# Layer norm of the first half rewritten, two-input sums redistributed over VectorE and GpSimd, and a new order of steps

## The chip, the cores and the metric

The kernel runs on one core of one Trainium2 chip, as a single launch. The metric is device time in microseconds (us) from the start to the end of the execution. The time of the kernel before is the median of 3 runs, 2762.42 us (2761.38 to 2765.03). All views of the profile come from one more execution, which took 2765.32 us.

## The reference, cut to what matters

There are 64 graphs of 256 nodes with 512 features. Everything is fp32: x is [64, 256, 512], adj [64, 256, 256], nodemask [64, 256], and each weight matrix has 512 rows. Two residual layers follow each other, each ended by a layer norm:

```python
def _gcn_layer(x, adj, W, b):
    return adj @ (x @ W) + b
h = relu(_gcn_layer(x, adj, W1, b1))
h = relu(_gcn_layer(h, adj, W2, b2))
x = _layernorm(x + _gcn_layer(h, adj, W3, b3))      # first half

q, k = jnp.split(x @ Wqk, 2, axis=-1)
v = x @ Wv
agg = adj @ (k * mask[:, :, None])
w = inv_scale * mask * (q * agg).sum(-1)            # one score for each node
x = _layernorm(x + softmax(w, axis=1)[:, :, None] * v)   # second half
```

`_layernorm` subtracts the mean of a row and divides by the root of its variance plus 1e-5; it has neither gain nor offset.

## The kernel before

*Pairs and products.* The graphs are handled as 32 pairs (`NPAIR`; `PAIR` = `G` = 2). Every large product is one level of a Strassen-Winograd scheme with seven products in place of eight: `seven` (L104) gives their order, 1, 7, 6, 2, 5, 4, 3, and says which PSUM bank each goes into and which sums are made after it. What the products need as operands are sums and differences of quarter blocks. These are the many small two-input operations of the kernel. The products from PSUM are combined by VectorE (`add`, L53; `sub`, L56) after ScalarE has copied one of the two to a buffer `tmp` (L109), or after `add` has made that `tmp` with another operand.

*Where the two-input sums run.* `unit` (L62) sends a sum to VectorE if its name is in the list `ON_DVE`, to GpSimd otherwise. A name is the owner and the number of the sum: h17 is S7 of layer 1's output (made from hT after the relu), h23 is S3 of layer 2's output, c2T6 and c2T7 are sums of the second layer's `support` results (buffers `sup`), x3, x5, x6 and x7 the sums S of the next pair's xT, and x4 to x7 also the sums T of the masked xm; a3 to a7 are sums of the adjacency, b3 the sum of x and the third layer's bias.

*The stages of a pair.*

- F, `front`: three times `support` (L290, the activations by W) and between them `aggregate` (L331, the adjacency), with bias and relu on ScalarE (L322) and the first sums S of the relu's result after it (`a_sums`). At its end it issues the loads of the mask and of x (1 MB, L85).
- S, `sums`: the three sums S of the next pair's xT, the four sums x + b3 (x<-x,b3b), the four sums of the next adjacency.
- B, `back`, for the pair before: the third aggregation (`adj_times`, L367), which makes the residual r and its statistics (mvt holds mean and variance); then `inv_std` (L371), the layer norm, the transposition of r in blocks of 32 x 32 by VectorE (L488, buffer tr), its way over DRAM (tr to via, via to x1T: five DMAs), and the sums T of xm (`t_sums`).
- G, `gather`: the adjacency by xm, into gt. M, `attention`: four copies and sums Z of x1T, the sums I of those on GpSimd (L59), and 49 products (L546) with blocks of Wv and of M = Wq Wk^T. These come from DRAM through a ring of seven buffers; the next fetch is issued after each product. The results R are combined by VectorE, v<-R makes v, and `score` (L563) makes w from gt.
- E, `finish`, for the pair before that: the softmax, v = v * s + r (L603), statistics, layer norm (ScalarE, L619) and the two stores out<-v (L622).

*What sets the order.* The kernel is written as generators, each of which gives a piece of its stage at a time. The loop over i = 0 to 32 interleaves F and S of pair i, B, G and M of pair i - 1 and E of pair i - 2. Which generator gives its next piece is a string of letters written by hand: `START` for i = 0, `ORDER` for i = 1 to 30, `LAST` for 31 and `END` for 32. With `manual_schedule` each engine's queue (TensorE, VectorE, ScalarE, GpSimd, and SyncE, which issues all DMAs) holds its instructions in the order in which they are written. So a string decides what stands ahead of what on every engine.

*The layer norm of the first half.* `inv_std` returns rs, one over the root of the variance, and nb = -mean * rs. From these `back` makes mrs = rs * ISCALE * mask and mnb = nb * ISCALE * mask. For each of the four (h, g) blocks of 128 x 512, ScalarE writes xm = r * mrs + mnb to another buffer (L460), and VectorE then turns r in place into r * rs + nb (L462), which may only overwrite r when ScalarE has read it. In the last pair (`end`) r is transposed by TensorE (L478), after 20 warming matmuls, and not over DRAM.

*Buffers that the text speaks of.* x and xm share one buffer (tag "x", one copy), R takes the places of T, x1T and Z, there is one v, two hT, five tmp, nine sup, six S and eight PSUM banks.

Of the kernel before, what the change touches and what calls it, by code (L numbers as in the profile page):

```python
# [9 lines left out]
FP = mybir.dt.float32  # L10
AF = mybir.ActivationFunctionType
OP = mybir.AluOpType
AX = mybir.AxisListType

P = 128
PAIR = 2
G = PAIR
# [3 lines left out]
def gcn_then_graph_attention(ctx: ExitStack, tc: tile.TileContext, xT, xN, adjT, mask, W1, b1, W2, b2, W3, b3,  # L21
                             WqT, WkT, Wv, out):

    nc = tc.nc
    NPAIR = xT.shape[0]
    N, D = 256, 512
    NH, DC = N // P, D // P
    HD = D // 2
    EPS = 1e-5
    ISCALE = 1.0 / math.sqrt(D)  # L30
# [1 line left out]
    SUP = 9  # L32
    SBUFS = 6
    TMP = 5
    ON_DVE = ('a5', 'c2T5', 'c2T6', 'c3T6', 'c3T7', 'h13', 'h23', 'h27', 'x3', 'x5')

    const = ctx.enter_context(tc.tile_pool(name="const", bufs=1))
    pool = ctx.enter_context(tc.tile_pool(name="work", bufs=1))
    small = ctx.enter_context(tc.tile_pool(name="small", bufs=2))
# [12 lines left out]
    def add(o, a, b):  # L52
        nc.vector.tensor_tensor(o, a, b, op=OP.add)  # L53
# [7 lines left out]
    def unit(name, o, a, b, op=OP.add):  # L61
        (nc.vector if name in ON_DVE else nc.gpsimd).tensor_tensor(o, a, b, op=op)  # L62

# [307 lines left out]
    def inv_std(mvt, n=G):  # L371

        sd = small.tile([P, NH, n], FP, name="sd")
        nc.scalar.activation(sd, mvt[:, :, :, 1], AF.Sqrt, bias=eps)  # L374
        rs = small.tile([P, NH, n], FP, name="rs")
        nc.vector.reciprocal(rs, sd)  # L376
        nb = small.tile([P, NH, n], FP, name="nb")
        nc.vector.scalar_tensor_tensor(nb, mvt[:, :, :, 0], -1.0, rs, op0=OP.mult, op1=OP.mult)  # L378
        return rs, nb

    def softmax_rows(w, gs):

# [50 lines left out]
    def back(i, C, aS, x, mask_t, end, put):  # L433
        r = pool.tile([P, G, NH, D], FP, name="r", tag="xT" if end else "r", bufs=1)
        xb = lambda h, j: x[:, :, h, j * HD:(j + 1) * HD]
        rb = lambda h, j: r[:, :, h, j * HD:(j + 1) * HD]
        st = small.tile([P, NH, G, 6], FP, name="st")
        mvt = small.tile([P, NH, G, 2], FP, name="mvt")

        def block(o, a, b, h=None):  # L440
            add(o, a, b)
            if h is not None:
                for g in range(G):
                    nc.vector.bn_stats(st[:, h, g], r[:, g, h, :])
                for g in range(G):
                    nc.vector.bn_aggr(mvt[:, h, g], st[:, h, g])
        yield from adj_times(aS, C, lambda y, t: add(rb(0, 1), y, t), lambda x: block(rb(0, 0), x, xb(0, 0), 0),
                             lambda v, t: block(rb(1, 1), v, t, 1), lambda v, t: add(rb(1, 0), v, t),
                             plus=(xb(0, 1), xb(1, 1), xb(1, 0)))

        rs, nb = inv_std(mvt)
        yield
        mrs = small.tile([P, NH, G], FP, name="mrs")
        nc.vector.scalar_tensor_tensor(mrs, rs, ISCALE, mask_t, op0=OP.mult, op1=OP.mult)
        mnb = small.tile([P, NH, G], FP, name="mnb")
        nc.vector.scalar_tensor_tensor(mnb, nb, ISCALE, mask_t, op0=OP.mult, op1=OP.mult)
        xm = pool.tile([P, G, NH, D], FP, name="xm", tag="x", bufs=1)

        def apply(h, g):
            nc.scalar.activation(xm[:, g, h, :], r[:, g, h, :], AF.Identity, scale=mrs[:, h, g:g + 1],  # L460
                                 bias=mnb[:, h, g:g + 1])
            nc.vector.tensor_scalar(r[:, g, h, :], r[:, g, h, :], rs[:, h, g:g + 1], nb[:, h, g:g + 1],  # L462
                                    op0=OP.mult, op1=OP.add)
        hg = [(h, g) for h in range(NH) for g in range(G)]
        xmb = [[xm[:, :, h, j * HD:(j + 1) * HD] for j in range(2)] for h in range(2)]
        if end:
            warm(20)
            x1T = [pool.tile([P, 2, G, N], FP, name="x1T", tag="act", bufs=2) for _ in range(2)]
            x1b = lambda h, k: x1T[k][:, :, :, h * P:(h + 1) * P]
            for h, g in hg:  # L470
                apply(h, g)
            yield
            xS = t_sums(xmb)
            for h, g in hg:
                yield
                pt = bank((P, 2, 2, P))
                for c in range(DC):
                    nc.tensor.transpose(pt[:, c // 2, c % 2], r[:, g, h, c * P:(c + 1) * P], ident)  # L478
                for k in range(2):
                    (nc.scalar.copy if h else nc.vector.tensor_copy)(x1T[k][:, :, g, h * P:(h + 1) * P], pt[:, k])  # L480
        else:
            tr = pool.tile([P, 4, 32, NH, 2, 2, G], FP, name="tr", tag="gt", bufs=1)
            x1T = pool.tile([P, P, NH, 2, 2, G], FP, name="x1T", bufs=1)
            x1b = lambda h, k: x1T[:, :, h, k].rearrange("p n c g -> p c g n")
            for h, g in hg:
                apply(h, g)
                for k in range(2):
                    nc.vector.transpose(tr[:, :, :, h, k, :, g].rearrange("p q j c -> p c q j"),  # L488
                                        r[:, g, h, k * HD:(k + 1) * HD].rearrange("p (c q j) -> p c q j", c=2, q=4))
                yield  # L490
            via = dram.tile([4, P, D], FP, name="via")
            nc.sync.dma_start(via.rearrange("q p e -> p q e"), tr.rearrange("p q j h k c g -> p q (j h k c g)"))
            for q in range(4):
                nc.sync.dma_start(x1T[q * 32:(q + 1) * 32].rearrange("p (a j) h k c g -> p a (j h k c g)", a=4),
                                  via[q].rearrange("(a i) e -> i a e", a=4))
            yield
            xS = t_sums(xmb)
        yield
        gt = pool.tile([P, NH, G, D], FP, name="gt", tag="gt", bufs=1)
        gb = lambda h, j: gt[:, h, :, j * HD:(j + 1) * HD]  # L500

        def gather():
            steps = adj_times(aS, xS, lambda y, t: add(gb(0, 0), y, t), lambda x: nc.scalar.copy(gb(0, 1), x),
                              lambda v, t: add(gb(1, 0), v, t), lambda v, t: add(gb(1, 1), v, t))
            for n, _ in enumerate(steps):
                if n == 6:
                    put["gt"] = gt
                    if i + 2 < NPAIR:
                        aTs[i + 2] = load_adj(i + 2)
                yield  # L510
        put["G"] = gather()
        w = small.tile([P, NH, G], FP, name="w", bufs=2)
        put["M"] = attention(i, x1b, w, r, mask_t, put)
# [80 lines left out]
    def finish(i, prev, gs=range(G)):  # L594

        r, v, w = prev
        n = len(gs)
        softmax_rows(w, gs)
        yield
        s = softmax_cols(gs)  # L600
        for k, g in enumerate(gs):
            for h in range(NH):
                nc.vector.scalar_tensor_tensor(v[:, g, h], v[:, g, h], s[:, h, k:k + 1], r[:, g, h, :],  # L603
                                               op0=OP.mult, op1=OP.add)
        yield
        st = small.tile([P, NH, n, 6], FP, name="st")
        mvt = small.tile([P, NH, n, 2], FP, name="mvt")
        for k, g in enumerate(gs):
            for h in range(NH):
                nc.vector.bn_stats(st[:, h, k], v[:, g, h])  # L610
                yield
        for k in range(n):
            for h in range(NH):
                nc.vector.bn_aggr(mvt[:, h, k], st[:, h, k])  # L614
        rs, nb = inv_std(mvt, n)
        yield
        for k, g in enumerate(gs):
            for h in range(NH):
                nc.scalar.activation(v[:, g, h], v[:, g, h], AF.Identity, scale=rs[:, h, k:k + 1],  # L619
                                     bias=nb[:, h, k:k + 1])  # L620
                yield
            nc.sync.dma_start(out[i, :, g * NH * D:(g + 1) * NH * D].rearrange("p (h f) -> p h f", h=NH), v[:, g])  # L622

    ORDER = ("BBFEFFBEBFBFBFBFFFBEFFFFBFSFBBBFFFBBBFGFFGGFFGFEEGMFFGMMMEGMMSFFMEMMEMMEFESMMEEFFMSM"
             "SMMMFMMMMFFEMMMMMMMMSMMMMMMFSMMMSSMMSSM")
    START = ("FFFBFBBFFBFBBBBBFFFFFFBBBBBFBBBBBBBBBBBFFBBBBSBFFBSBFBBFFFBBFBBFBFSFBFFBBBBFBBSFFBSB"
             "BSFBSFFSBBBSBBBBBSFBBBBBSBSBB")
    LAST = ("FBBSEFBFEBBFFBFBFBFFBFFFFEBBFFBBFBFBEFEEGFEGGFFEGEFFMMGSFFGMMMMFEFMMMMEMMMMMMEMMMFMM"
            "GSMMMMEMMMMMMMMFMMMSSMMMFMSSSFMFFSFSFSM")
    END = ("BEBBBBBBEBBBBBBBBGMGMEMMBEGGEEMGEGEMMMMMMEMEEMEMMMMMMMMMMMGMMBMMMMMMMMMMXMMXXMMMXYXM"  # L630
           "XMYXYMYYMYXYMYXYBMYMMXXYYXM")

    def run(order, rest, **gens):
        res = {}
# [81 lines left out]
```

## Time and profile before

| | |
|---|---|
| median of 3 runs | 2762.42 us (2761.38 to 2765.03) |
| the profiled execution | 2765.32 us |
| its span, first to last instruction on the core | 2763.5 us |
| mean TensorE clock granted, as a share of the full one | 0.996 |
| instructions | 41007 |
| DMA | 403.7 MB, 146 GB/s on the mean |
| VectorE transposes tr<-r (L488) | 248, 606 ns each |
| GpSimd sums x<-x,b3b (L62) | 128, 1523 ns each |
| GpSimd sums sup<-sup (L62) | 160, 1372 ns each |
| VectorE sums R<-ps,tmp (L53) | 384, 616 ns each |
| ScalarE copies tmp<-ps (L109) | 768, 584 ns each |

The engines are PE (TensorE's matmuls), PEld (its loading of weights, beside the matmuls), DVE (VectorE), ACT (ScalarE), POOL (GpSimd) and SP (SyncE, which issues DMAs; SPq is its queue). A group of instructions is written as line, engine, operation, output<-inputs. A timeline line gives the start in us from the start of the span, the us from the first start to the last end, the group and how many instructions it holds, and in brackets the idle time of the engine just before it with what ended it. A waits line gives the group that waited, what ended the wait, and the total, the times and the longest, in us. [...]

### The profile page before, as it was taken

What the parts mean: (1) busy time and instruction counts of PE and PEld (TensorE: products, weight loads), DVE (VectorE), ACT (ScalarE), POOL (GpSimd) and SP (SyncE); (2) the same over time, 40 slices, a digit from 0 to 9 for tenths busy, and PEclk for the clock granted to TensorE, in tenths of its full rate; (3) what the DMA queues carried; (4) which work ended last, traced back from release to release, by engine and by line L of the source; (5) the groups of instructions that cost most, each with busy time, mean ns of one, the idle gap of its engine ahead of it and who ended that gap; (6) DMA issues with size and microseconds to landing.
All of it is one profiled execution on the core that took longest, in us unless ns stands there. A gap on an engine that the chain in (4) does not pass through costs nothing. (4 is left out here: it accounts for less than half of the span.)

```text
span 2763.5 us, 41007 instructions
## 1 busy us (share of the span) xinstructions
PE 2716.9 (98%) x14290; PEld 2401.7 (87%) x14290; DVE 2145.0 (78%) x3828; ACT 1133.1 (41%) x2050; POOL 1262.8 (46%) x966
## 2 busy tenths in 40 slices
PE   9999999999999999999999999999999999999996
PEld 8888888888888888888888888888888888888885
DVE  5778777877777777778777777877787877778777
ACT  3434344434344343443334443434433444434343
POOL 3535455444554354544445543445544455434442
PEclk9999999999999999999999999999999999999998
DMA  6534554344544445543455444455434554434553
GB/s 209 165 110 147 165 175 135 117 143 154 163 151 123 126 147 162 173 135 112 143 162 162 141 129 131 147 162 176 133 115 141 161 162 148 130 123 147 162 155 97
DMA packets 202233, 403.71 MB, mean 146 GB/s; under 512 B 24752, under 2 KB 61872, under 8 KB 193968
## 3 DMA queue, kind: packets, MB, share of 16 engines
q1 hardware_dynamic: 202032, 401.10, 46.5%
q8 instruction: 117, 1.92, 0.3%
q14 instruction: 84, 0.69, 0.1%
HBM read 328.54 MB, written 72.48 MB: 145 GB/s over the span
## 5 line engine op out<-in xcount | busy, mean ns | idle before, releaser
L109 ACT COPY tmp<-ps 128x512 f32<-128x512 f32 x768 | 431.3, 584 | 643.3 <-PE ps L290 257.1
L62 POOL TENSOR_TENSOR sup<-sup 128x512 f32<-128x512 f32 x160 | 218.1, 1372 | 565.9 <-DVE sup L53 409.2
L546 PE MATMUL ps<-ring,I 128*128 128x256 f32 x1792 | 433.0, 381 | 7.7 <-DVE tmp L53 3.0
L546 PEld LDWEIGHTS ps<-ring,I 128*128 128x128 f32 x1792 | 334.1, 190 | 66.3 <-DVE R L53 11.7
L290 PE MATMUL ps<-w_T,S 128*128 128x256 f32 x1536 | 351.0, 381 | 9.2 <-POOL S L62 7.6
L301 ACT COPY sup<-ps 128x512 f32<-128x512 f32 x96 | 56.2, 586 | 722.2 <-PE ps L290 722.2
L290 PEld LDWEIGHTS ps<-w_T,S 128*128 128x128 f32 x1536 | 286.7, 190 | 59.7 <-POOL S L62 20.5
L546 PE MATMUL ps<-ring,Z 128*128 128x256 f32 x1344 | 327.9, 380 | 1.1 <-ACT Z L524 1.1
L59 POOL TENSOR_TENSOR I<-Z 128x384 f32<-128x384 f32 (+1 forms) x128 | 190.1, 1504 | 244.5 <-DVE Z L527 150.8
L546 PEld LDWEIGHTS ps<-ring,Z 128*128 128x128 f32 x1344 | 254.4, 190 | 38.4 <-ACT Z L524 3.3
L331 PEld LDWEIGHTS ps<-aT,sup 128*128 128x128 f32 x2048 | 253.5, 192 | 13.2 <-issue 6.6
L331 PE MATMUL ps<-aT,sup 128*128 128x128 f32 x2048 | 261.8, 276 | 1.8
L53 DVE TENSOR_TENSOR R<-ps,tmp 128x512 f32<-128x512 f32 (+1 forms) x384 | 221.2, 616 | 48.7 <-PE ps L546 48.4
L62 POOL TENSOR_TENSOR x<-x,b3b 128x512 f32<-128x512 f32 x128 | 192.2, 1523 | 128.7 <-DMA x<-in_xN 119.3
L290 PE MATMUL ps<-w,hT 128*128 128x256 f32 x1024 | 242.0, 379 | 0.0
L290 PE MATMUL ps<-w_T,hT 128*128 128x256 f32 x1024 | 236.5, 379 | 0.0
L290 PEld LDWEIGHTS ps<-w_T,hT 128*128 128x128 f32 x1024 | 194.6, 190 | 26.5
L53 DVE TENSOR_TENSOR sup<-ps,tmp 128x512 f32<-128x512 f32 x288 | 192.8, 677 | 30.8 <-PE ps L290 30.7
L290 PEld LDWEIGHTS ps<-w,hT 128*128 128x128 f32 x1024 | 192.0, 190 | 24.7
L331 PE MATMUL ps<-aS,sup 128*128 128x128 f32 x1536 | 206.3, 279 | 1.7 <-ACT tmp L109 1.1
L322 ACT ACTIVATE hT<-hT,b 128x256 f32<-128x256 f32 x384 | 167.4, 501 | 87.1 <-DVE hT L53 86.2
L331 PEld LDWEIGHTS ps<-aS,sup 128*128 128x128 f32 x1536 | 188.9, 192 | 11.4 <-DVE hT L53 4.8
(116 smaller groups left out, 4762.8 us busy)
## 6 DMA issues: line engine op xcount, KB each, us to landing
ring<-mv SPq DMA_DIRECT2D x672, 256.0 KB, 3.6
x<-in_xN SPq DMA_DIRECT2D x32, 1024.0 KB, 8.0
out<-v SPq DMA_DIRECT2D x64, 512.0 KB, 7.6
xT<-in_xT SPq DMA_DIRECT2D x31, 1024.0 KB, 5.0
via<-tr SPq DMA_DIRECT2D x31, 1024.0 KB, 4.2
x1T<-via SPq DMA_DIRECT2D x124, 256.0 KB, 4.7
ring<-mv SPq DMA_DIRECT2D x224, 128.0 KB, 3.1
aT<-in_adjT SPq DMA_DIRECT2D x32, 512.0 KB, 3.9
```

What stands on the lines that cost most here:

```text
L53: nc.vector.tensor_tensor(o, a, b, op=OP.add)
L59: (nc.gpsimd).tensor_tensor(o, a, b, op=op)
L62: (nc.vector if name in ON_DVE else nc.gpsimd).tensor_tensor(o, a, b, op=op)
L109: nc.scalar.copy(t, ps)
L290: nc.tensor.matmul(ps[:, g], lhsT=src[n][:, c, g], rhs=w[n][:, c], start=(first and g == 0 and c == 0), stop=(g == G - 1 and c == 1), skip ...
L301: nc.scalar.copy(C[2], x)
L322: nc.scalar.activation(o[:, c], (o if ps is None else ps)[:, c], AF.Relu, bias=b[:, 2 - 2 * j + c:3 - 2 * j + c])
L331: nc.tensor.matmul(ps[:, c, g], lhsT=C[n][:, g, c * P:(c + 1) * P], rhs=aS[n][:, g], start=(first and c == 0 and g == 0), stop=(c == 1 and ...
L546: nc.tensor.matmul(ps[:, k], lhsT=left[n](place[o]), rhs=wt[:, k], start=(first and k == 0), stop=(k == len(outer) - 1), skip_group_check= ...
```

## The change

The layer norm's second form: VectorE first turns r in place into (r - mean) * rs, with the mean straight from mvt, and ScalarE then makes xm = r * ms from the result, ms = mask * ISCALE. `inv_std` no longer makes nb; `finish`, which still needs it, makes its own; mrs and mnb are gone. `ON_DVE` gains b3, c2T7, h17, h25 and h26, and loses h13, h23, x3 and x5 (which names two sums a pair, one of xT and one of xm). All four order strings are new. The numbers of buffers are the same. In the changed kernel, lines between `inv_std` and `finish` stand one or two lower than before: the layer norm's r is L456, xm L460, the ring's matmuls L545.

```diff
@@ -32,7 +32,7 @@
     SUP = 9
     SBUFS = 6
     TMP = 5
-    ON_DVE = ('a5', 'c2T5', 'c2T6', 'c3T6', 'c3T7', 'h13', 'h23', 'h27', 'x3', 'x5')
+    ON_DVE = ('a5', 'b3', 'c2T5', 'c2T6', 'c2T7', 'c3T6', 'c3T7', 'h17', 'h25', 'h26', 'h27')
 
     const = ctx.enter_context(tc.tile_pool(name="const", bufs=1))
     pool = ctx.enter_context(tc.tile_pool(name="work", bufs=1))
@@ -374,9 +374,7 @@
         nc.scalar.activation(sd, mvt[:, :, :, 1], AF.Sqrt, bias=eps)
         rs = small.tile([P, NH, n], FP, name="rs")
         nc.vector.reciprocal(rs, sd)
-        nb = small.tile([P, NH, n], FP, name="nb")
-        nc.vector.scalar_tensor_tensor(nb, mvt[:, :, :, 0], -1.0, rs, op0=OP.mult, op1=OP.mult)
-        return rs, nb
+        return rs
 
     def softmax_rows(w, gs):
 
@@ -448,19 +446,18 @@
                              lambda v, t: block(rb(1, 1), v, t, 1), lambda v, t: add(rb(1, 0), v, t),
                              plus=(xb(0, 1), xb(1, 1), xb(1, 0)))
 
-        rs, nb = inv_std(mvt)
-        yield
-        mrs = small.tile([P, NH, G], FP, name="mrs")
-        nc.vector.scalar_tensor_tensor(mrs, rs, ISCALE, mask_t, op0=OP.mult, op1=OP.mult)
-        mnb = small.tile([P, NH, G], FP, name="mnb")
-        nc.vector.scalar_tensor_tensor(mnb, nb, ISCALE, mask_t, op0=OP.mult, op1=OP.mult)
+        ms = small.tile([P, NH, G], FP, name="ms")
+        nc.vector.tensor_scalar(ms, mask_t, ISCALE, None, op0=OP.mult)
+        rs = inv_std(mvt)
+        yield
         xm = pool.tile([P, G, NH, D], FP, name="xm", tag="x", bufs=1)
 
-        def apply(h, g):
-            nc.scalar.activation(xm[:, g, h, :], r[:, g, h, :], AF.Identity, scale=mrs[:, h, g:g + 1],
-                                 bias=mnb[:, h, g:g + 1])
-            nc.vector.tensor_scalar(r[:, g, h, :], r[:, g, h, :], rs[:, h, g:g + 1], nb[:, h, g:g + 1],
-                                    op0=OP.mult, op1=OP.add)
+        def turn(h, g):
+            nc.vector.tensor_scalar(r[:, g, h, :], r[:, g, h, :], mvt[:, h, g, 0:1], rs[:, h, g:g + 1],
+                                    op0=OP.subtract, op1=OP.mult)
+
+        def masked(h, g):
+            nc.scalar.activation(xm[:, g, h, :], r[:, g, h, :], AF.Identity, scale=ms[:, h, g:g + 1])
         hg = [(h, g) for h in range(NH) for g in range(G)]
         xmb = [[xm[:, :, h, j * HD:(j + 1) * HD] for j in range(2)] for h in range(2)]
         if end:
@@ -468,7 +465,8 @@
             x1T = [pool.tile([P, 2, G, N], FP, name="x1T", tag="act", bufs=2) for _ in range(2)]
             x1b = lambda h, k: x1T[k][:, :, :, h * P:(h + 1) * P]
             for h, g in hg:
-                apply(h, g)
+                turn(h, g)
+                masked(h, g)
             yield
             xS = t_sums(xmb)
             for h, g in hg:
@@ -483,7 +481,8 @@
             x1T = pool.tile([P, P, NH, 2, 2, G], FP, name="x1T", bufs=1)
             x1b = lambda h, k: x1T[:, :, h, k].rearrange("p n c g -> p c g n")
             for h, g in hg:
-                apply(h, g)
+                turn(h, g)
+                masked(h, g)
                 for k in range(2):
                     nc.vector.transpose(tr[:, :, :, h, k, :, g].rearrange("p q j c -> p c q j"),
                                         r[:, g, h, k * HD:(k + 1) * HD].rearrange("p (c q j) -> p c q j", c=2, q=4))
@@ -612,7 +611,9 @@
         for k in range(n):
             for h in range(NH):
                 nc.vector.bn_aggr(mvt[:, h, k], st[:, h, k])
-        rs, nb = inv_std(mvt, n)
+        rs = inv_std(mvt, n)
+        nb = small.tile([P, NH, n], FP, name="nb")
+        nc.vector.scalar_tensor_tensor(nb, mvt[:, :, :, 0], -1.0, rs, op0=OP.mult, op1=OP.mult)
         yield
         for k, g in enumerate(gs):
             for h in range(NH):
@@ -621,14 +622,14 @@
                 yield
             nc.sync.dma_start(out[i, :, g * NH * D:(g + 1) * NH * D].rearrange("p (h f) -> p h f", h=NH), v[:, g])
 
-    ORDER = ("BBFEFFBEBFBFBFBFFFBEFFFFBFSFBBBFFFBBBFGFFGGFFGFEEGMFFGMMMEGMMSFFMEMMEMMEFESMMEEFFMSM"
-             "SMMMFMMMMFFEMMMMMMMMSMMMMMMFSMMMSSMMSSM")
-    START = ("FFFBFBBFFBFBBBBBFFFFFFBBBBBFBBBBBBBBBBBFFBBBBSBFFBSBFBBFFFBBFBBFBFSFBFFBBBBFBBSFFBSB"
-             "BSFBSFFSBBBSBBBBBSFBBBBBSBSBB")
-    LAST = ("FBBSEFBFEBBFFBFBFBFFBFFFFEBBFFBBFBFBEFEEGFEGGFFEGEFFMMGSFFGMMMMFEFMMMMEMMMMMMEMMMFMM"
-            "GSMMMMEMMMMMMMMFMMMSSMMMFMSSSFMFFSFSFSM")
-    END = ("BEBBBBBBEBBBBBBBBGMGMEMMBEGGEEMGEGEMMMMMMEMEEMEMMMMMMMMMMMGMMBMMMMMMMMMMXMMXXMMMXYXM"
-           "XMYXYMYYMYXYMYXYBMYMMXXYYXM")
+    ORDER = ("BBFEFFBEBFFBBFEBEFEEFFBSFFFFFBFBFFBBBBEFFBEGFGEFGFFEGSGFMFGMMGMFMFMMFMSMMMEMFMMSMSMM"
+             "FSMFSSEMMSSFFMESMFMMMMMMMMMMMMMMMMMMMMF")
+    START = ("FBFFFBFBFBFBBBBBFFFFFFBBFBBBBSBFBBBBBBFFBFBBFBBBFBFFFBSBBSBBFBFBFFFFBFBBBBFSBSBFBFBB"
+             "FBBBBSBBBBBBSSBBSSFBBSBSBBBBB")
+    LAST = ("FBBEFBSFEBBFFBSFEBFFEBFFBFFFFSFFBBBEFBEFBBGGFEEGFFGEFMGEFFFMGMMMMFMFMMMMMMMEMEMMMMMM"
+            "MFGMMMMMMFMMMMMMMFMFSSMMMSFFSMSSMEFFSMS")
+    END = ("BBBBBBBBBBBBEBEBBMGMGGEGEMGEMMMEEBGMBMMMMEEEEMEMMBMMMGMMMMMMMMMMMMMMMMMMMXMMXXMMMXYX"
+           "YMXYXYYXMXMXXMYYYYYMYMMMXYM")
 
     def run(order, rest, **gens):
         res = {}
```

## The prediction

> **What bounds the kernel now.** I read the page's first part, then the waits, the DMA issues and the timeline of one step. TensorE is never far from full:
>
> ```profile
> PE 2716.9 (98%) x14290; PEld 2401.7 (87%) x14290; DVE 2145.0 (78%) x3828; ACT 1133.1 (41%) x2050; POOL 1262.8 (46%) x966
> ```
>
> 98% is flattered by overlapping matmuls, so I count starts. In the timeline 16 passes of 256 columns take 3.45 us (904.90 to 908.35, below), 0.216 each; a matmul is two passes, 0.432. Passes of 128 columns start 0.112 apart. A steady step (one pair of graphs) has 161 matmuls of 256 columns and 56 of 128: 161 x 0.432 + 56 x 0.224 = 82.1 us, with the softmax transposes 82.7. The x loads of L85 start between 63.3 and 2681.0, 31 steps of 84.4. So TensorE loses 1.7 us a step, some 53 us in all: no reordering can gain more. What it waits for:
>
> ```profile
> POOL x L62 <- DMA x<-in_xN: 119.3, 29, 22.4
> ...
> PEld ps L290 <- POOL S L62: 20.5, 32, 0.8
> ...
> PEld ps L546 <- DVE R L53: 12.4, 30, 0.9
> ...
> PE ps L290 <- POOL S L62: 7.6, 32, 0.4
> ```
>
> (The columns are total, times, longest.) TensorE has two regular losses: it waits for a sum S on GpSimd (L62) after the relu, and for VectorE in the second half's products (L546). In the gaps between matmul starts, less 0.216, they come to 0.50 and 0.42 us a step on the mean of 29 steps; the rest, some 0.8, are short waits at bank turns. The first line costs nothing now, since GpSimd has time. One step of the timeline, for SyncE, GpSimd, VectorE and TensorE:
>
> ```profile
> 892.67 0.33 SPq L85 DMA_DIRECT2D x<-in_xN  x1
> ```
> ```profile
> 901.89 5.68 POOL L62 TENSOR_TENSOR x<-x,b3b 128x512 f32<-128x512 f32 x3 [4.42 <-DMA x<-in_xN]
> ```
> ```profile
> 904.76 1.68 DVE L582 TENSOR_TENSOR R<-R 128x1024 f32<-128x1024 f32 x1
> 906.37 2.29 DVE L53 TENSOR_TENSOR v<-R 128x1024 f32<-128x1024 f32 x1
> 908.58 1.01 DVE L53 TENSOR_TENSOR tmp<-ps,R 128x512 f32<-128x512 f32 x2
> ```
> ```profile
> 904.90 3.62 PE L290 MATMUL ps<-w_T,hT 128*128 128x256 f32 x16
> 908.35 2.75 PE L546 MATMUL ps<-ring,I 128*128 128x256 f32 x12
> 910.94 1.46 PE L546 MATMUL ps<-ring,Z 128*128 128x256 f32 x6
> 912.90 1.56 PE L546 MATMUL ps<-ring,I 128*128 128x256 f32 x6 [0.50 <-DVE tmp L53]
> ```
>
> See that x arrives 9 us after its issue, that VectorE then runs without a gap, and that TensorE meets its result 0.5 us early.
>
> [...] GpSimd stands 4.42 us before its first x. [...] beside an idle GpSimd the sum of two 1024-element operands takes 1.21 us, above 1.68 and 2.29; S<-xT,S goes from 0.68 to 1.74. [...] L462 takes 0.55 alone, a sum 0.69.
>
> **The change part by part.** The built program's order gives each queue; t is counted from the third of the four matmuls with W3's first block, near which x is issued.
>
> *Layer norm.* Gone are nb, mrs, mnb (0.166 + 0.153 + 0.156), new is ms (0 to 0.16, I take 0.15 from mrs's row): VectorE -0.3 us a step. The new L456 has L462's shape and operand kinds; I take its price, 0.55, between 0.46 and 1.66 by what GpSimd does. VectorE no longer waits for ScalarE's xm (49.8 us in all, 1.6 a step); xm waits for r instead, and the first product of xm is 7 us off. What is late next: `finish`'s four bn_aggr, root, rs and nb now stand behind the eight transposes on VectorE, and behind the root on ScalarE a PSUM copy that TensorE needs 18 matmuls after its first S, 8.8 us after the relu. From the relu: the sum 0.65, four L456 and eight transposes (0.49 apart) with two short waits for GpSimd 6.6, bn_aggr 0.4, root 0.3, copy 0.6: 8.5. Cost 0, with 0.3 to spare; if each L456 met a GpSimd operation the row would end 1 us later and 0.7 would stall. tr and its DMA come 1 us sooner than now.
>
> *The lists.* VectorE gets the four x + b3b (0.69 each, c3T's sums of the same shape; 0.67 alone to 1.74 beside GpSimd), c2T7 (0.71), h17 (0.98; 0.69 to 1.0), h25 (0.74, from xT's in-place row; 0.69 to 1.74) and h26 (0.67): 5.9. It gives away h13, h23 (0.67 each), x3 (1.68) and both x5 (0.74, 0.67): 4.4. With the layer norm it has 1.1 us more a step, and GpSimd by the same sum of its rows 4.7 less. Load decides nothing here (67 and 39 of 84 us); place does.
>
> h17: now the relu ends, S takes 1.27 on GpSimd, TensorE waits 0.40 and 0.10:
>
> ```profile
> 945.47 1.27 POOL L62 TENSOR_TENSOR S<-hT 128x512 f32<-128x512 f32 x1 [5.11 <-ACT hT L322]
> 946.81 1.35 POOL L62 TENSOR_TENSOR S<-hT,S 128x512 f32<-128x512 f32 x1
> ```
>
> On VectorE 0.69 to 1.0, directly behind the relu and ahead of L456: the sum ends 0.3 us before the matmul, or with it. Gain 0.50 (at least 0.35).
>
> *The x adds.* SyncE issues x behind a ring fetch that waits for the last matmul before W3's (its end: t = -0.7); now x follows that fetch by 0.96 us, so t = 0.3. The table of DMAs gives 8.0 us to landing (L85: 6.6 to 9.1); the fetch ahead is 128 KB, not 256, so I take 7.8, and t = 8.1. On VectorE the first add stands right behind two R sums that end by t = 3.5. VectorE idles 4.6 us, and behind it queue, in order: R<-ps, three adds, both R<-R, v, aT, three sup sums, tmp, the T7, T6 pair, and the R sums. Starts of 512-element operations are 0.60 apart, of 1024 1.13 (GpSimd is idle by t = 7), of 256 0.34. Up to aT: 5 x 0.60 + 3 x 1.13 + 0.34 = 6.7. From there 14 operations; now 13 of them run from 908.58 to 915.76, 7.2, plus one 0.60: 7.8. TensorE meets this queue three times (a tmp for matmul 38, banks for 44 and 50). The R sum for the last ends at 8.1 + 0.1 + 6.7 + 7.8 = 22.7. TensorE would be there at 50 x 0.432 = 21.6. Stall 1.1 us, in place of 0.42: cost 0.7. Both ends: x at 7.0, none (gain 0.42); x at 9.4, 2.4 (cost 2.0).
>
> *Other DMAs.* One of the two out<-v moves 12 us ahead of x, to just before the adjacency load; 1 MB is drained by then. The other stays behind x and lands some 3.9 us after it (now 3.5), 1.4 before v<-R needs its buffer. aS follows aT on GpSimd and is needed a step later. Cost 0; if an out came ahead of x, its 1.25 us would go into the stall.
>
> *Products after the transposes.* The first products with Z are interleaved otherwise with layer two's aggregate; their copies stand behind relus on ScalarE. With x1T 1 us sooner all come in time (0); without, I count 0.15 at an hT and 0.25 at a copy. I take 0.15.
>
> A step: 0.7 - 0.5 + 0.15 = +0.35; 30 steps, +11.
>
> *Last pair.* Now TensorE stands before the last transposes:
>
> ```profile
> 2709.52 2.79 PE L478 MATMUL ps<-ident,r 128*128 128x128 f32 x12 [3.34 <-DVE r L462]
> ```
>
> because four v sums (2.74 us) and xm go before r. In the new order r follows rs at once, under the 20 warm matmuls (4.6 us): -3.7; but exp of the softmax now stands behind four xm there, about 1.7 late. -2. The first pair, where x also holds VectorE, about +1 (0 to 3).
>
> Sum: 11 - 2 + 1 = +10 on the profiled execution's 2765.3, 2775.5 (2 us lie outside its span of 2763.5). It ran 2.9 above the median, so 2773 in terms of the median 2762.42.
>
> **The rivals.** *x in time.* If x lands by t = 7.0, VectorE keeps up, and what is left is h17 and the end: 30 x (0.15 - 0.50 - 0.42) - 1 = -24, 2738; with x at 7.3 on the mean the stall is 0.3 and the time 2747, which I take. Against: 8.0 is the median, 6.6 the least of 32. For: fewer bytes ahead. It decides (0.2% faster) once the mean stall is below 0.62, x by t = 7.6.
>
> *x late and the norm late.* x at 8.7 (stall 1.7, cost 1.3), L456 held by GpSimd (0.5): 30 x (1.3 - 0.5 + 0.5) - 1 = +38, 2800. For: x in this step took 9.1. Against: the unchanged ring fetches, and GpSimd has less to do.
>
> *It washes out.* The losses are moved, TensorE keeps its 1.7 us: 2762.
>
> **How the numbers follow.** The measurement tells 0.2% (5.5 us) from no change. Forecast 2773 (0.47, between 2766 and 2785), x in time 2747 (0.2), late 2800 (0.23), washed out 2762 (0.1). Slower: 0.42 of the first and 0.23, 0.65; same: 0.05 and 0.1, 0.15; faster 0.2. For 8 in 10 I leave out a tenth on each side: 2748 to 2806. The slower cases' own range is 2768 to 2806.
>
> **What would show it.** Right: VectorE's longest wait is for the DMA of x, 4 to 5 us a step, and GpSimd's is gone; TensorE's waits for POOL S vanish; its waits for DVE R and tmp at the products grow to about 1.1 us a step; DVE waits for xm are gone; at the end PE waits for e_t, not for r. Wrong: x waits under 3.5 us, or no growth at the products; or growing waits elsewhere, for ScalarE's copies.

## The result and the profile after

The changed kernel takes 2737.33 us (median of 5 runs, 2736.07 to 2740.82), the kernel before 2765.03 us (median of 5 runs, 2761.38 to 2769.49). The ratio is 0.9902, with a 95% interval of 0.9887 to 0.9917: faster by 1%, where I had forecast 0.4% slower. The time lies beside the rival "x in time" as it was worked out with x landing by t = 7.0 (2738), and outside the stated range.

The page of the changed kernel, first part:

```profile
PE 2707.0 (99%) x14290; PEld 2406.4 (88%) x14290; DVE 2190.8 (80%) x3860; ACT 1130.6 (41%) x2050; POOL 1123.5 (41%) x870
```

VectorE is busy 46 us longer and the kernel is still faster: its load decided nothing. The waits of the changed kernel (total, times, longest in us), those of TensorE and the one for x:

```profile
DVE x L62 <- DMA x<-in_xN: 100.1, 32, 4.4
...
PE ps L398 <- DVE e_t L392: 5.5, 2, 3.6
...
PEld ps L545 <- DVE tmp L53: 4.0, 9, 0.5
...
PEld ps L545 <- DVE R L53: 2.7, 3, 1.4
```
```profile
PE ps L290 <- POOL S L62: 0.4, 1, 0.4
```

VectorE does stand before x, as forecast, but 3.1 us a step, not 4.6. Of TensorE's 32 waits for POOL S at L290 one is left (0.4 us), of its 30 for DVE R three. The timeline of the same step as in the prediction, first SyncE, then VectorE:

```profile
885.05 0.38 SPq L85 DMA_DIRECT2D x<-in_xN  x1
886.76 4.48 SPq L215 DMA_DIRECT2D ring<-mv  x5
891.33 0.38 SPq L623 DMA_DIRECT2D out<-v  x1
```
```profile
890.96 0.69 DVE L62 TENSOR_TENSOR x<-x,b3b 128x512 f32<-128x512 f32 x1 [2.64 <-DMA x<-in_xN]
...
893.37 1.22 DVE L53 TENSOR_TENSOR R<-R 128x1024 f32<-128x1024 f32 x1
...
895.10 1.22 DVE L581 TENSOR_TENSOR R<-R 128x1024 f32<-128x1024 f32 x1
896.24 1.22 DVE L53 TENSOR_TENSOR v<-R 128x1024 f32<-128x1024 f32 x1
```

See two things. x is used 5.9 us after its issue (9.2 before), and no store follows it for 6 us. The three long sums run at their price beside an idle GpSimd, 1.22, where before the second and third took 1.68 and 2.29.

The layer norm's row on VectorE (four norm instructions and eight transposes behind the relu), its first and last lines in the changed kernel and its last in the kernel before, in the step of the prediction's lines:

```profile
935.96 0.69 DVE L62 TENSOR_TENSOR S<-hT 128x512 f32<-128x512 f32 x1 [1.01 <-ACT hT L322]
936.57 0.54 DVE L456 TENSOR_SCALAR r<-r,mvt,rs 128x512 f32<-128x512 f32 x1
...
941.43 1.06 DVE L487 STREAM_TRANSPOSE tr<-r 128x256 f32<-128x256 f32 x2
```
```profile
952.56 1.05 DVE L488 STREAM_TRANSPOSE tr<-r 128x256 f32<-128x256 f32 x2
```

h17 (S<-hT) now takes 0.69 us on VectorE, directly behind the relu, where GpSimd took 1.27.

TensorE's gaps tell where the time came from. As in the prediction, a gap is the time between the starts of two matmul passes less the nominal (a matmul of 256 columns stands in the records as two passes, each over all 256: 5376 passes at L290 for the program's 2688 matmuls), and the table has means over 29 steady steps. Here every gap over 0.04 us counts, step by step. The 0.42 of the prediction, and the 0.16 for the changed kernel that some expectations name, keep only the places where the mean is over 0.04; the full count at the products is 0.48 and 0.29.

| us a step | first S (h17) | second S, or the copy before it | work behind the row of norm and transposes | second half's products | elsewhere |
|---|---|---|---|---|---|
| before | 0.50 | 0 | 0 | 0.48 | 0.06 |
| changed | 0 | 0 | 0 | 0.29 | 0 |
| e2_b3pool | 0 | 0 | 0 | 2.72 | 0 |
| e4_h17 | 0 | 0.45 | 0.73 | 0.42 | 0.12 |
| e5_hold_again | 0 | 0 | 0 | 1.78 | 0 |
| e6_oldnorm | 0 | 0 | 1.74 | 0.37 | 0.05 |
| e7_newnorm | 0.50 | 0 | 0 | 0.49 | 0 |
| e9_norm_h17 | 0 | 0.67 | 0.05 | 0.46 | 0 |
| e10_h17pool | 0.53 | 0 | 0 | 0.31 | 0 |
| e11_b3pool_adj | 0 | 0 | 0 | 0.26 | 0 |
| e12_all_but_order | 0 | 0.65 | 0.07 | 0.13 | 1.65 |

A row's sum, with 82.59 us of matmuls and 0.77 to 0.79 of bank turns, gives the length of that kernel's mean step to within 0.03 us, so the table leaves no other wait out.

The steady steps went from 84.40 to 83.65 us on the mean: 29 x 0.75 = 21.6. The stretch ahead of them gives 2.7, the one behind them 0.3 (with the four passes that the new order does earlier counted where they were). In all 24.6, the difference of the two spans.

### The profile page after: what moved, and what is told of

Read it like the earlier page. It is cut to its first block, busy times and chain, and to the rows that moved or that the text cites. A ratio compares the mean times of both kernels' runs of the same rounds, so it can differ in the third digit from the quotient of the medians.

```text
span 2738.9 us, 41013 instructions
## 1 busy us (share of the span) xinstructions
PE 2707.0 (99%) x14290; PEld 2406.4 (88%) x14290; DVE 2190.8 (80%) x3860; ACT 1130.6 (41%) x2050; POOL 1123.5 (41%) x870
## 5 line engine op out<-in xcount | busy, mean ns | idle before, releaser
L62 POOL TENSOR_TENSOR sup<-sup 128x512 f32<-128x512 f32 x128 | 177.4, 1397 | 796.1 <-DVE sup L53 715.6
L545 PE MATMUL ps<-ring,I 128*128 128x256 f32 x1792 | 431.9, 380 | 4.3 <-DMA ring<-mv 1.7
L545 PEld LDWEIGHTS ps<-ring,I 128*128 128x128 f32 x1792 | 332.7, 190 | 57.0 <-issue 10.3
L290 PE MATMUL ps<-w_T,S 128*128 128x256 f32 x1536 | 348.0, 379 | 0.4 <-POOL S L62 0.4
L545 PE MATMUL ps<-ring,Z 128*128 128x256 f32 x1344 | 326.6, 379 | 1.5 <-DVE R L53 1.2
L290 PEld LDWEIGHTS ps<-w_T,S 128*128 128x128 f32 x1536 | 287.5, 190 | 41.9 <-POOL S L62 0.8
L545 PEld LDWEIGHTS ps<-ring,Z 128*128 128x128 f32 x1344 | 252.7, 190 | 35.7 <-DVE R L53 2.7
L53 DVE TENSOR_TENSOR R<-ps,tmp 128x512 f32<-128x512 f32 (+1 forms) x384 | 221.8, 615 | 35.5 <-PE ps L545 31.3
L53 DVE TENSOR_TENSOR sup<-ps,tmp 128x512 f32<-128x512 f32 x288 | 191.5, 681 | 67.0 <-PE ps L290 65.3
L290 PE MATMUL ps<-w,hT 128*128 128x256 f32 x1024 | 242.0, 379 | 0.0
L290 PE MATMUL ps<-w_T,hT 128*128 128x256 f32 x1024 | 241.4, 379 | 0.0
L290 PEld LDWEIGHTS ps<-w_T,hT 128*128 128x128 f32 x1024 | 194.6, 190 | 26.5
L290 PEld LDWEIGHTS ps<-w,hT 128*128 128x128 f32 x1024 | 192.0, 190 | 24.7
L62 POOL TENSOR_TENSOR S<-hT,S 128x512 f32<-128x512 f32 x96 | 136.2, 1419 | 184.1 <-DVE S L62 182.5
```

The costliest lines, as they stand in the source:

```text
L290: nc.tensor.matmul(ps[:, g], lhsT=src[n][:, c, g], rhs=w[n][:, c], start=(first and g == 0 and c == 0), stop=(g == G - 1 and c == 1), skip ...
L545: nc.tensor.matmul(ps[:, k], lhsT=left[n](place[o]), rhs=wt[:, k], start=(first and k == 0), stop=(k == len(outer) - 1), skip_group_check= ...
```

## The experiments

Theory after the result: TensorE gains 0.50 from h17 and 0.19 at the products, each by itself; x is in time because no store stands close behind it. Rivals: x comes sooner for another reason; one part (h17, the form, the place of x + b3) brings all of the gain. The first four runs refuted "each by itself", and the rest test in its place that form, list and order are worth this only together.

**A store behind x.** In `finish` the first store of a pair, in the steady steps, is held until `load_x`:

```diff
+            if k == 0 and i < NPAIR - 3:
+                held.append(store)
+            else:
+                store()
...
 def load_x(i):
...
         nc.sync.dma_start(t, xN[i]...)
+        while held:
+            held.pop()()
```

> The changed kernel with one difference: in the steady steps the first of the two stores out<-v of a pair isn't issued where it stands (12 us ahead of the x load) but right behind the x load, as a store stands in the kernel before. Theory (x is in time because no store shares the DMA engines with it): x lands 7.5 to 8.5 us after its issue, not 6.5; VectorE's wait for it grows from 3.1 to 4 us or more a step; TensorE stands 0.9 to 1.3 us a step at the second half's products; 2737 + 28 x 0.9 = 2762, between 2754 and 2770. Rival (x lands sooner for another reason, such as the ring fetches ahead of it): landing 6.5 and 2737, within 3.

Measured: median 2771.5 of 11 runs, 1.0020 of the kernel before (1.0008 to 1.0032). Of these the profiled one took 10108 us, with matmuls of 1105 ns (ring,I) where the changed kernel has 380, at a granted clock of 1.000; no run here shows why, and nothing but one landing of x, further down, is read from it. The other ten lie between 2759 and 2778. The same kernel, profiled in a further execution:

> The kernel of e1_hold once more, for a profile of an ordinary execution. Theory: x lands 7.5 to 8.5 us after its issue (6.5 in the changed kernel), VectorE waits 4 us or more a step for it, and TensorE's gaps in the second half's products come to 0.9 to 1.3 us a step. Rival: the landing is as in the changed kernel, and the 30 us that e1_hold was longer lie somewhere else, such as in v<-R, which waits for the stores.

Measured: 2784.4, one execution, longer than any of those ten. The landing of x and the waits in this run's profile (POOL aS is no operand of these matmuls: this wait is for several semaphores, and in each long gap a tmp of VectorE, L53, ends last, 0.10 us before the matmul, aS 0.29 before):

```profile
x<-in_xN SPq DMA_DIRECT2D x32, 1024.0 KB, 8.4
```
```profile
DVE x L62 <- DMA x<-in_xN: 150.9, 32, 6.4
...
PEld ps L549 <- POOL aS L62: 37.0, 23, 2.5
...
PE ps L549 <- POOL aS L62: 28.5, 21, 2.2
```

VectorE waits 4.7 us a step for x and TensorE 1.78 at the products, more than the 0.9 to 1.3 expected: the theory holds, the rival falls (v<-R waits for a store 3 times, 2.5 us in all). The ten other executions, some 34 us above the changed kernel, would have about 1.2 us a step more than its 0.29 (an estimate: 34 over 29 steps). Step by step the stall follows x: in the changed kernel, when x lands at t = 7.4 to 7.6 (t as in the prediction), it is 0.55 to 0.71, at 7.90 it is 1.04; in e5_hold_again 1.33 at 8.18 and 2.48 at 9.33. Four steps of each lie above this line, by up to 1.4 us, for other reasons.

What stands behind x bears on its landing. In e5_hold_again the store's place is the only difference from the changed kernel. Mean over 27 steps of the issue of the next store after x, and x's landing:

| | next store | x lands |
|---|---|---|
| e5_hold_again | +0.46 us | 8.19 us |
| before | +1.59 | 8.10 |
| e3_newlist | +4.82 | 6.94 |
| changed | +5.61 | 6.41 |

The transfers ahead of x land alike in the four (the last ring fetch at 2.2 to 2.6).

The packet records of the traces show a part of how a later store can do this. x moves in 128 packets of 8 KB, a store in packets of 4 KB. From 2 to 4 us after x's issue its packets take 0.44 us on the mean in e5_hold_again and 0.46 in the kernel before, against 0.33 in the changed kernel; yet in none of these steps has a packet of a store started by then (the first at 4.0 us). So the store does not overtake x: x's own packets take longer. Why is not shown. From 4 us on, packets of x and of a store are under way together in the kernel before, for 3.3 us a step, with 15.9 packets of all kinds at a time on the mean, on the page's 16 DMA engines. Nor is a store behind x enough by itself: in the profiled execution of e1_hold, where only one ring fetch is still under way at x's issue and none follows within 8 us, x lands after 5.9 us with the store at +0.46.

**x + b3 on GpSimd**, all else as changed:

```diff
-    ON_DVE = ('a5', 'b3', 'c2T5', ...
+    ON_DVE = ('a5', 'c2T5', ...
```

> The changed kernel with the four sums x + b3 a pair back on GpSimd. Theory (on GpSimd they lengthen VectorE's sums of two SBUF operands beside them, so their place on VectorE pays even though VectorE then waits for x): R<-R and v<-R rise from 1.22 to 1.6 to 2.3 us and TensorE's stalls at the products from 0.16 to 0.3 to 0.45 us a step: 2741 to 2746. Rival (VectorE's wait for x is a cost, which this takes away): the stalls go to 0 and the time to 2731 to 2734.

Measured: 2814.6, 1.0182 of before (1.0168 to 1.0195): 77 us more than the changed kernel, and neither theory had it. The timeline of one step, GpSimd and VectorE:

```profile
911.38 5.68 POOL L62 TENSOR_TENSOR x<-x,b3b 128x512 f32<-128x512 f32 x3 [4.49 <-DMA x<-in_xN]
917.02 2.25 POOL L62 TENSOR_TENSOR S<-hT,S 128x512 f32<-128x512 f32 x1
919.23 1.27 POOL L62 TENSOR_TENSOR x<-x,b3b 128x512 f32<-128x512 f32 x1
920.46 0.72 POOL L62 TENSOR_TENSOR aS<-aT 128x256 f32<-128x256 f32 x1
```
```profile
916.48 1.67 DVE L53 TENSOR_TENSOR v<-R 128x1024 f32<-128x1024 f32 x1 [0.54 <-DMA out<-v]
921.21 0.43 DVE L62 TENSOR_TENSOR aT<-aT 128x256 f32<-128x256 f32 x1 [3.07 <-POOL aS L62]
```

aT is summed in place on VectorE (a5), so it waits for GpSimd's aS (a7), which reads it, and that now stands behind x. VectorE idles 3.07 us with the tmp sums behind it, and TensorE loses 2.72 a step at the products. With the adjacency's sums ahead of x + b3 in `sums`, that queue is gone:

```diff
+        if i + 1 < NPAIR:
+            yield from adj_sums(aTs[i + 1], put)
+            yield
         x = put["x"]
...
-        if i + 1 < NPAIR:
-            yield from adj_sums(aTs[i + 1], put)
```

> The changed kernel with x + b3 on GpSimd, as in e2_b3pool, but with the sums of the adjacency ahead of them in the stage's steps, so that VectorE's aT sum no longer waits for a GpSimd sum behind x (in e2_b3pool aS ended at 16.2 us of the step and VectorE stood until then). Theory (e2_b3pool was slow through that queue alone): its stall of 1.8 us at the products goes; what is left is what GpSimd's sums do to VectorE's beside them, 0 to 0.4 a step: 2735 to 2750. Rival (the x sums on GpSimd cost by themselves): 2790 or more.

Measured: 2744.3, 0.9927 (0.9907 to 0.9948), the same as the changed kernel within the intervals. So where x + b3 runs is not the gain; it must only have nothing behind it that is urgent.

**Parts of the change on the kernel before.** First the new list alone, in the old order:

```diff
-    ON_DVE = ('a5', 'c2T5', 'c2T6', 'c3T6', 'c3T7', 'h13', 'h23', 'h27', 'x3', 'x5')
+    ON_DVE = ('a5', 'b3', 'c2T5', 'c2T6', 'c2T7', 'c3T6', 'c3T7', 'h17', 'h25', 'h26', 'h27')
```

> The kernel before with the changed list of sums on VectorE alone (old order, old layer norm): the x sums are on VectorE, and both stores stand right behind the x load. Theory (a late x behind which VectorE's queue stands costs TensorE time): x lands at 8 to 9, VectorE waits 4 to 5 us a step for it, the stalls at the products grow from 0.42 to 1 to 2 us while h17's 0.50 goes: 30 x (1.5 - 0.42 - 0.5) = +17 on the kernel before, 2765 to 2800. Rival (VectorE has room for the wait; h17 is all that counts): 2750 or less.

Measured: 2837.8, 1.0268 (1.0254 to 1.0282). Slow, but not by the theory: VectorE waits for x only 3 times in all (6.9 us), since in this order its first x sum comes at t = 9.1 behind other work, after x is there (7.2 on the mean). The loss lies elsewhere: gaps before a ring product at W3 (0.79), before the second S products of two layers (0.53 and 0.43), before the softmax (0.35) and at late ring products (0.72). This run tells nothing on a late x; e5_hold_again does.

h17 alone:

```diff
-    ON_DVE = ('a5', ..., 'h13', 'h23', ...
+    ON_DVE = ('a5', ..., 'h13', 'h17', 'h23', ...
```

> The kernel before with h17 alone added to VectorE's list. Theory (the 0.50 us a step before the second layer's first S product is GpSimd's 1.27 us for S7 and nothing else): TensorE's waits for POOL S go, 31 x 0.5 = -15.5: 2749.5 where the kernel before has 2765. Rival (the wait moves to the next sum or to VectorE's later work): 2758 to 2766.

Measured: 2785.9, 1.0079 (1.0065 to 1.0092): slower, the theory falls. The wait for S is gone, but:

```profile
PEld ps L290 <- DVE sup L53: 27.3, 31, 1.4
...
PE ps L290 <- DVE sup L53: 14.9, 31, 1.0
...
PE ps L290 <- ACT tmp L109: 6.4, 30, 0.3
```

Ahead of mrs and mnb, S holds xm, xm holds ScalarE's queue (two relus and a copy, 0.45 at the second S) and VectorE's row: from the relu's end to the last transpose 9.22 us on the mean where the kernel before has 8.22. The sup sum behind the row comes 0.73 late.

The form alone (`inv_std` and `finish` as in the changed kernel):

```diff
-            nc.scalar.activation(xm..., r..., AF.Identity, scale=mrs..., bias=mnb...)
-            nc.vector.tensor_scalar(r..., r..., rs..., nb..., op0=OP.mult, op1=OP.add)
+            nc.vector.tensor_scalar(r..., r..., mvt..., rs..., op0=OP.subtract, op1=OP.mult)
+            nc.scalar.activation(xm..., r..., AF.Identity, scale=ms...)
```

> The kernel before with the new form of the layer norm alone, old list and old order. Theory (in the old order nothing that TensorE waits for stands close behind the row; a shorter row is room that the list has to use): TensorE's 0.50 at POOL S and 0.42 at the products stay; 2765 less 0 to 5, the last pair's wait for r included. Rival (the new form itself brings the gain): 2745 or less.

Measured: 2761.3, 0.9987 (0.9981 to 0.9994), as the theory had it. The row ends 5.6 us after the relu, and nothing uses that: 0.50 at the first S and 0.49 at the products stay.

Both these edits, the form and h17, in the old order:

> The kernel before with the new form of the layer norm and h17 on VectorE, old order. In e4_h17 (old form) the gain of 0.50 us a step was lost three times over: the row of norm and transposes ended 0.7 later and a sum behind it was 0.70 late, and on ScalarE xm, waiting behind S, held two relus and a copy, 0.44. Theory: with the new form the row is at least 0.7 shorter, so the 0.70 goes; but xm still stands ahead of the relus on ScalarE and now waits for S and r, so the 0.44 stays or grows to 0.8. A step: -0.5 + 0.4 to 0.8 on e7_newnorm's 2761: 2758 to 2770. Rival (form and h17 together are the gain, no order needed): 2747 or less.

Measured: 2771.2, 1.0024 (1.0015 to 1.0033). The row ends after 6.6, the 0.73 is gone but for 0.05, ScalarE's copy costs 0.67. The 29 steady steps are 5.6 us longer than those of e7_newnorm; the other 4 of the 9.9 between the medians lie outside them (in the two profiles it is 8.6, all behind the steady steps) and are not explained. The rival falls.

The form and the whole new list, the old order:

> The kernel before with the new form and the new list, all but the new order. Theory (form and list need the order): most of e3_newlist's 2838 stays, less what the shorter row gives, 0.3 to 1.2 a step: 2800 to 2830. Rival (the form was what e3_newlist lacked): 2765 or less.

Measured: 2829.2, 1.0239 (1.0214 to 1.0263): with everything but the order the kernel is 92 us slower than with it.

**Parts taken from the changed kernel.** The diff of the form turned round, in the new order and list:

```diff
-            nc.vector.tensor_scalar(r..., r..., mvt..., rs..., op0=OP.subtract, op1=OP.mult)
-            nc.scalar.activation(xm..., r..., AF.Identity, scale=ms...)
+            nc.scalar.activation(xm..., r..., AF.Identity, scale=mrs..., bias=mnb...)
+            nc.vector.tensor_scalar(r..., r..., rs..., nb..., op0=OP.mult, op1=OP.add)
```

> The changed kernel with the old form of the layer norm (ScalarE reads r first, VectorE then overwrites it), its new order and list kept. Theory (the new form matters because VectorE's row of four norm instructions and eight transposes, 5.9 us in the changed kernel and 8.3 before, stands between the relu and what TensorE needs next): the row is 1 to 2.3 us longer, what stands behind it is late by 0.5 to 1.5 us a step, and the time is 2755 to 2785. Rival (the form is worth nothing by itself, as I had predicted): 2737, within 4.

Measured: 2798.9, 1.0121 (1.0107 to 1.0134), 61 us above the changed kernel and more than the 2755 to 2785 expected. In its waits:

```profile
ACT sd L374 <- DVE mvt L614: 89.5, 31, 3.1
...
PEld ps L290 <- ACT tmp L109: 54.4, 29, 1.9
...
PE ps L290 <- ACT tmp L109: 42.8, 29, 1.5
```

The row ends 9.35 us after the relu instead of 6.57; `finish`'s bn_aggr behind it, its root on ScalarE behind that (89.5 us of waits; 14.0 in the changed kernel), and the copy behind the root keep TensorE 1.74 us a step.

And h17 on GpSimd:

```diff
-    ON_DVE = (..., 'c3T7', 'h17', 'h25', 'h26', 'h27')
+    ON_DVE = (..., 'c3T7', 'h25', 'h26', 'h27')
```

> The changed kernel with h17 back on GpSimd. Theory: TensorE waits for POOL S again, 0.40 to 0.55 us a step, and S6, which follows it on GpSimd, comes 0.6 later, with less than 0.4 to spare, so up to 0.3 more: 2737 + 30 x 0.4 to 0.8 = 2749 to 2761. Rival (in the new order h17 isn't critical): 2737, within 4.

Measured: 2756.6, 0.9973 (0.9964 to 0.9982), 19 us above the changed kernel. TensorE waits for POOL S again, 0.53 a step, the second S is in time:

```profile
PEld ps L290 <- POOL S L62: 21.7, 32, 0.8
...
PE ps L290 <- POOL S L62: 8.8, 32, 0.4
```

**An attempt at more.** The x load in two halves, and in `END` the softmax's second piece later:

```diff
+        for g in range(G):
+            nc.sync.dma_start(t[:, g], src[:, g])
-    END = ("BBBBBBBBBBBBEBEBBMGMGGEG...
+    END = ("BBBBBBBBBBBBEBBBMGMEGGEG...
```

> The changed kernel with the x load issued as two halves, one for each graph, and in the last pair the softmax's second piece put behind the last four transposes and the first gather products. Theory (VectorE's wait for x still costs the 0.16 us a step at the products; TensorE's 3.77 us there fills with other work): x's first half lands 1.5 us sooner, gaps at the products below 0.05, 30 x 0.13 + 2 to 3 = 6 to 7: 2730 to 2732. Rival (both halves share the DMA engines and land together; the last pair's wait moves on to another place): 2735 to 2739.

Measured: 2740.5, 0.9908 (0.9893 to 0.9923): no different from the changed kernel. VectorE waits 1.9 us a step for x (58.1 us in all, 3.1 before), but the products keep 0.21, in 8 of the 29 steps (up to 1.18 at one place). The steady steps gain 1.8 us in the profiles and what follows them loses 2.9. No version here beats the changed kernel.

## Why the prediction was wrong, step by step

- *x adds: the step that failed.* The working had TensorE at the products wait 22.7 - 21.6 = 1.1 us, from x landing at t = 8.1. x landed at t = 6.7 on the mean, and the stall was 0.29. The 7.8 us to landing was taken from the table of the kernel before, corrected for a smaller fetch ahead. What had made it 8.0 stood behind x, as e5_hold_again shows: a store, there 1.6 us later. I had followed both stores, one "12 us ahead of x", the other "behind x", and priced only what is ahead. No later store overtakes x: in the kernel before, the next one lands at least 1.23 us behind it in each of the 29 steady steps. But that order tells nothing of how long x's own packets take (0.33 or 0.44 us), and that is where the time went. The chain behind x was right: its sum puts the onset of the stall at t = 7.0, and in the changed kernel the stall of most steps grows from t = 6.9 on, us for us. With x at t = 8.4 (e5_hold_again) the same sum gives 22.7 + 0.3 - 21.6 = 1.4, and 1.78 was measured, though most of it at the first of the three places where TensorE meets the queue, not at the last. The case "x at 7.0, none" was named, and given 0.2. But a mean landing is not enough for the sum: at 6.7 it gives no stall, while the 29 landings spread from 5.5 to 7.9, and the nine at 7.4 or later make 0.22 of the 0.29.
- *h17.* Gain 0.50 right (0.53 when taken back, e10_h17pool). That it could be added to the rest was wrong in principle: alone it costs 21 us (e4_h17), with the form alone in the old order 10 over the form (e9_norm_h17).
- *Layer norm, cost 0.* From the relu to the last transpose I had 0.65 + 6.6 = 7.25; measured 6.57, since L456 takes 0.49 on the mean, not 0.55, and waits for GpSimd don't come. The copy behind the root makes no gap: cost 0 is right. But the step measured the form against the old kernel, where it is worth 3.7 us (e7_newnorm). In the new queue it carries 61 us (e6_oldnorm), through the very chain that the prediction names.
- *Products after the transposes, 0.15.* No gap there: cost 0. A step is then 0.29 - 0.48 - 0.50 - 0.06 = -0.75, as measured; the 0.06, at later products, was not in the sum.
- *Last pair, -2; first pair, +1.* Measured -0.3 and -2.7. The last pair's new wait is the one forecast, for e_t; it is 3.6 us long, not 1.7. In the first pair x holds nothing up. (2765.3 + 10 is 2775.3, not 2775.5; nothing hangs on it.)

That the time falls on the rival's 2738 is in part luck. That sum has no stall at the products, 0.15 behind the transposes and -1 for the ends; measured are 0.29, 0 and -3.

That GpSimd's sums lengthen VectorE's, read from the kernel before (1.21 us beside an idle GpSimd, 1.68 and 2.29 beside a busy one), holds: in e11_b3pool_adj R<-R takes 1.71 and v<-R 1.84 beside GpSimd, in e2_b3pool the two R<-R 1.51 and 1.85 and v<-R 1.74 on the mean, against 1.22 in the changed kernel. But it doesn't decide here: the products' gap of that run is 0.26.

Left open: which moves in `ORDER` bring the 92 us that e12_all_but_order lacks (gaps in four places), and what h13, h23, x3, x5, h25, h26 and c2T7 do in the list; none of these was tried singly. Nor was the new order run with the old list and form, or form and order with the old list: that the three are worth this only together rests on taking single parts out, and on form and list without the order.

## What to carry to other kernels

A transfer's time in the profile hung here on its neighbours in time, one issued behind it among them (x landed after 8.19 us with the next store at +0.46, after 6.41 with it at +5.61): before carrying a landing time over to a new order, list what is issued from the fetch ahead to the landing, in both orders. In a kernel whose engines each work through one written queue, price a moved operation by what stands behind it on its engine, and be ready for the parts of such a change to be worth nothing, or less, one at a time. Taking a part out of the finished change shows what it carries; adding it to the old kernel shows only whether there was room.

## What the runs showed of the hardware that I had not expected

After TensorE had stood for 3.56 us near the end, its next matmuls ran at half speed. The stretches of the changed kernel's last pair around a wait of 3.56 us (the columns: stretch; its length; busy us and instructions of PE, PEld, DVE, ACT and POOL; granted clock, DMA share, GB/s), and the timeline behind it:

```profile
2670.00:2679.00 9.00, 8.85 (x62) 7.67 (x61) 8.32 (x20) 1.11 (x3) 0.00 (x0) 1.00 0.01 2
2679.00:2684.00 5.00, 1.44 (x12) 1.19 (x11) 2.93 (x9) 4.11 (x8) 3.09 (x3) 0.96 0.00 0
2684.00:2690.00 6.00, 6.00 (x18) 4.99 (x19) 5.24 (x8) 2.69 (x6) 1.92 (x2) 0.50 0.00 0
```
```profile
2683.60 0.98 PE L398 MATMUL ps<-ident,e_t 128*128 128x2 f32 x4 [3.56 <-DVE e_t L392]
...
2687.04 3.56 PE L367 MATMUL ps<-T,aS 128*128 128x256 f32 x8
```

Eight passes of 256 columns take 3.4 us from start to start, 0.42 each, twice the usual 0.216. The granted clock is 0.50 for 6.83 us, until 2690.4, so the wait costs some 3 us more than its length (an estimate, half of that time). The kernel before pays for its wait of 3.34 us with 3.41 us at 0.50. The length of the wait that brings this is not settled here. In e8_split_end 2.10 us were enough (0.54 over the next 6 us). In the kernel before, the clock falls to 0.50 at the end of a wait of 1.95 us (at 2746.4), while one of 1.87 us (to 2674.3) left it at 1.00. In e2_b3pool 23 of the steady steps have a wait of 1.3 to 2.0 us, and the clock fell in four of them, each time for 3.41 us (0.993 on the mean of that run, 0.995 in the changed kernel).
